# Layer norms in three steps over halved channels, a gate that normalises by tokens, and its tokens placed in three parts

## The chip, the cores and the metric

The kernel runs on one core of a Trainium2 chip. The core has a matrix engine (TensorE, PE in the profile; PEld is its loading of stationary operands), VectorE (DVE), ScalarE (ACT), GpSimd (POOL) and a sync engine (SP) that issues DMA transfers. Each engine runs its own queue of instructions in order, and semaphores make one wait for another. The metric is the device time of one execution in microseconds, the median over runs. All data is fp32.

## The reference

The input x is (2, 256, 48, 48): two images of 2,304 tokens with 256 channels, 4,608 tokens in all. Four blocks follow each other, each adding to x; what this case touches is the token-wise layer norm between them.

```python
def _ln_t(v, eps=1e-5):
    m = jnp.mean(v, axis=-1, keepdims=True)
    s = jnp.var(v, axis=-1, keepdims=True)
    return (v - m) / jnp.sqrt(s + eps)
...
    x = _L0_conv_ref(x, ...)                       # layer 0: selective scan, both directions
    x = x + _L1_conv_ref(_gn(x), ...)              # layer 1: linear attention, 3x3 convolution, MLP of 2048
    t = _to_tokens(x)
    t = t + _L2_attn_ref(_ln_t(t), ...)            # layer 2: attention of three thirds of the tokens
    t = t + _L2_ffn_ref(_ln_t(t), ...)             # 4 experts, two a token, weights from a graph
    t = t + _L3_attn_ref(_ln_t(t), L3_attn_q_weight)
    t = t + _L3_ffn_ref(_ln_t(t), ...)             # 8 experts, one a token
```

The last two, cut to what matters here:

```python
    query = jnp.einsum('bnd,de->bne', input, q_weight)
    att = jax.nn.sigmoid(jnp.einsum('bnd,bmd->bnm', query, input))
    value = jnp.einsum('bnm,bmd->bnd', att, input)
...
    logits = x @ gate_w + gate_b
    idx = jnp.argmax(probs, axis=-1)
    pos = (jnp.cumsum(one_hot, axis=0) * one_hot).sum(-1).astype(jnp.int32) - 1
    kept = pos < C                                 # C = 720 places an expert
    buf = jnp.zeros((E, C, D), dtype=h.dtype).at[idx, pos_safe].set(x, mode='drop')
```

So each token goes to its best expert, into the next free place there, in the order of the tokens. `pos` of a token depends on all tokens before it.

## The kernel before, in words

**Layout.** `E.xres`, the sum so far, and `E.xn`, its normalised copy, lie in SBUF as [128, 2, 4608]: channels on partitions in two halves of 128, tokens along the free axis. Work goes by chunks of W = 384 tokens, six a batch, twelve in all; where tokens lie on partitions, by tiles of 128 (NT = 36, three a chunk).

**The layer norm** (`layernorm`, L89 to L105; `normalize_piece` calls it for one chunk of xres into xn). As channels lie on partitions, the mean is a product with `mean_c`, a 128x128 matrix of 1/256, accumulated over the two halves (L95), which leaves the mean on every partition. VectorE subtracts it (L96), ScalarE squares (L98), two more products give the variance (L101), ScalarE takes the root (L103), VectorE the reciprocal (L104) and the product (L105). Layer 0 has a norm of its own, which isn't touched. `layernorm` runs 48 times.

**Where the norms stand.** In layer 1, `mlp(c, t1, midway)` works on one chunk in four groups g of the hidden size; `midway`, at g = 1, projects the next chunk and normalises the chunk before. Its xres comes from L646. Between chunks VectorE also sorts lists of graph edges (`sort_list`, L854 to L872). In layer 2's attention, the chunks of batch 0 are normalised two at the end of each of the three heads of batch 1; inside a head, a loop over six row tiles t makes scores (`sp`, L750), their maximum, Exp, the reciprocal of the sum, the scaled probabilities `pr` (L764) and their transposes (`tp`, L768). In layer 2's experts (`layer2_ffn`) six chunks are normalised at the start. Then expert pieces run beside the graph's work: for 8 of 12 chunks (`early`) the four experts' outputs go to DRAM (`y_d`), since the graph's weights aren't there yet. Afterwards a loop over the four other chunks takes `join` twice (it reads the pieces, VectorE weights them, GpSimd adds them into xres at L1399) with a norm after each, and `later(c)` once, which computes a chunk's experts and adds them (L1421), again with a norm.

**Layer 3's attention** (`layer3_attn`) runs, for each batch, six query chunks c against 18 key tiles i: two products `sp` (L1637), a Sigmoid (L1642), two products `po` (L1644), and at the end of a chunk L1650 adds `po` into xres. What stands in the list `behind` is issued then.

**The gate** follows the attention by chunks. `Gate.take(c)` normalises the chunk of xres into `gate_h`, transposes three tiles on TensorE with the gate's weights appended to the identity (`tg`, L1495), which gives normalised tokens and the logits' two halves in one, copies both out (L1498, L1499) and writes the tokens to DRAM (`xt_d`, L1501). `Gate.place(b)` then works on the 18 tiles of a batch: softmax, best expert, counts over tiles by two products and eight scans, and a table of which token lies in which of 8 x 720 places, built by one one-hot product a tile (`tb`, L1580, its operand `ol` from L1579). Batch 0's tiles are placed behind the first attention chunk of batch 1, batch 1's after the attention. The table's `token` (L1586) is what the first gather of layer 3's experts (`xe`, L1712, an indirect DMA by GpSimd) waits for.

The order of instructions on an engine is that of the program as a scheduler places it by data dependencies; tile pools with a fixed number of buffers set which instructions wait for an older tile's readers.

Of the kernel before, what the change touches and what calls it, by code (L numbers as in the profile page):

```python
# [8 lines left out]

# [8 lines left out]
F32 = mybir.dt.float32  # L18
# [70 lines left out]
def layernorm(E, wp, ps, src, dst, eps):  # L89

    nc = E.nc
    w = src.shape[2]
    mp = ps.tile([P, w], F32, tag="ln", name="ln_mean")
    for k in range(2):
        nc.tensor.matmul(mp, lhsT=E.mean_c, rhs=src[:, k, :], start=k == 0, stop=k == 1)  # L95
    nc.vector.tensor_tensor(dst, src, bc(mp, [P, 2, w], 1), ALU.subtract)  # L96
    sq = wp.tile([P, 2, w], F32, tag="ln_sq", name="ln_sq")
    nc.scalar.activation(sq, dst, AF.Square)  # L98
    vp = ps.tile([P, w], F32, tag="ln", name="ln_var")
    for k in range(2):  # L100
        nc.tensor.matmul(vp, lhsT=E.mean_c, rhs=sq[:, k, :], start=k == 0, stop=k == 1)  # L101
# [3 lines left out]
    nc.vector.tensor_tensor(dst, dst, bc(rs, [P, 2, w], 1), ALU.mult)  # L105

# [333 lines left out]
def normalize_piece(E, wp, ps, c, eps=1e-5):  # L440

    cs = slice(c * W, (c + 1) * W)
    layernorm(E, wp, ps, E.xres[:, :, cs], E.xn[:, :, cs], eps)
# [4 lines left out]
def layer1(ctx, E, edges):  # L448
# [78 lines left out]
    for b in range(NB):  # L527
# [79 lines left out]
        def mlp(c, t1, midway):  # L607
# [16 lines left out]
            for g in range(16 // FG):  # L624
# [3 lines left out]
                if g == 1:  # L628
                    midway()
                for m in range(2):  # L630
# [20 lines left out]
        for c in range(NCH):  # L651
# [5 lines left out]
            def midway():  # L657
                if dw is not None:
                    following.append(project(c + 1, dw))
                if b * NCH + c:  # L660
                    normalize_piece(E, lw, psn, b * NCH + c - 1)

            mlp(c, t1, midway)
# [6 lines left out]
    normalize_piece(E, lw, psn, NB * NCH - 1)  # L670
# [4 lines left out]
def layer2_attn(ctx, E):  # L675
# [46 lines left out]
    for b in range(NB):  # L722
# [8 lines left out]
        for h in range(NH):  # L731
# [11 lines left out]

            pT = act.tile([P, ST, S], F32, tag="pT", name="pT", bufs=1)
            for t in range(ST):
# [19 lines left out]
                for n in range(0, ST, 3):  # L765
# [5 lines left out]
                    else:  # L771
                        nc.vector.tensor_copy(pT[:, n : n + 3, t * P : (t + 1) * P], tp)

# [26 lines left out]

            if b:
                for c in range(2 * h, 2 * h + 2):
                    normalize_piece(E, wp, psn, (b - 1) * NCH + c)
# [499 lines left out]
def layer2_ffn(ctx, E, edges):  # L1303
# [25 lines left out]
    with (  # L1329
# [3 lines left out]
        for c in range(NCH, 2 * NCH):  # L1333
            normalize_piece(E, lw, psl, c)
# [66 lines left out]
    def later(c):  # L1401
# [6 lines left out]
        for e in range(NX):  # L1408
            gp = spread(gT, e)
            for hid in hidden(c, e):  # L1410
                pass
# [14 lines left out]
    for i in range(n_late):  # L1426
        while joined * n_late < EARLY * (i + 1):
            join(joined)
            normalize_piece(E, late, psn, joined)
            joined += 1  # L1430
        later(EARLY + i)
        if i < n_late - 1:
            normalize_piece(E, late, psn, EARLY + i)
# [3 lines left out]
class Gate:  # L1437

# [6 lines left out]
    def __init__(self, E, keep, wp):  # L1445
# [13 lines left out]
        self.lg = wp.tile([P, NT, 2, NX], F32, name="lg")  # L1459
# [23 lines left out]

    def take(self, E, c, lw, psl):

        nc = E.nc
        TG = self.TG
        h = lw.tile([P, 2, W], F32, tag="gate_h", name="gate_h")
        layernorm(E, lw, psl, E.xres[:, :, c * W : (c + 1) * W], h, 1e-5)
        xtok = lw.tile([P, TG, C], F32, tag="gate_x", name="gate_x", bufs=1)  # L1490
        for i in range(TG):
            o = slice(i * P, (i + 1) * P)
            xp = psl.tile([P, 2, P + self.NX], F32, tag="xp", name="xp", bufs=2)
            for k in range(2):
                nc.tensor.matmul(  # L1495
                    xp[:, k, :], lhsT=h[:, k, o], rhs=self.tg[:, k, :], start=True, stop=True
                )
            nc.vector.tensor_copy(xtok[:, i, :].rearrange("p (k m) -> p k m", k=2), xp[:, :, :P])  # L1498
            nc.vector.tensor_copy(self.lg[:, c * TG + i], xp[:, :, P:])  # L1499
# [3 lines left out]
        )  # L1503

    def place(self, E, b, ps):

        nc, wp = E.nc, self.wp
        NX, CAP, JT, JP, NJ = self.NX, self.CAP, self.JT, self.JP, self.NJ
        ids, ones = self.ids, self.ones
        n = NT // NB  # L1510
        bs = slice(b * n, (b + 1) * n)
        full = [P, n, NX]

        pb = wp.tile(full, F32, tag="pb", name="pb")
        nc.vector.tensor_tensor(pb, self.lg[:, bs, 0], self.lg[:, bs, 1], ALU.add)
        nc.vector.tensor_tensor(pb, pb, bc(self.gb, full, 1), ALU.add)
# [19 lines left out]
        pp = ps.tile(full, F32, tag="xp", name="pp", bufs=2)  # L1536
# [350 lines left out]
```

## Time and profile before

Three runs took 5549.81, 5555.41 and 5556.3 us. The profile is of one execution.

| what | value |
|---|---|
| median of three runs | 5555.41 us |
| the profiled execution's own time | 5556.52 us |
| its span in the profile | 5554.7 us |
| outside the span | 1.8 us |
| granted TensorE clock, mean over the span | 0.954 |
| TensorE busy | 4861.4 us (88%) |
| VectorE busy | 3476.2 us (63%) |
| ScalarE busy | 2380.4 us (43%) |
| GpSimd busy | 2388.5 us (43%) |

The page cuts the span in 40 slices of 139 us. Each digit is an engine's busy share in tenths, and `PEclk` the granted clock of TensorE in tenths of full speed:

```profile
PE   7888888887887787779999999998799999997996
DVE  4899988988999888999973234375624211212333
POOL 3888887888999888820000000078112000001112
PEclk8999999999999899999999999999899999998997
```

The first 17 slices are layer 0, where three engines share the work. Layer 1 follows up to slice 22, layer 2 with its graph up to slice 31 (GpSimd's 7 and 8 in slices 26 and 27 are the graph), layer 3's attention up to 36, its experts to the end. An engine's busy time includes time at half clock, which makes its matmuls take twice as long. The groups that are touched are small beside these: the 192 matmul records of `ln_mean` have a median of 486 ns each, and a pair of fp32 products leaves four such records.

### The profile page before, as it was taken

The page shows a single profiled execution, that of the slowest core. Times are in us where ns is not written, and L with a number is a line of the kernel's source. Part 1 is how long each engine was busy: PE and PEld are TensorE (multiplying, and loading weights), DVE is VectorE, ACT ScalarE, POOL GpSimd, SP SyncE. Part 2 cuts the span into 40 slices and gives each one's busy share as a digit, 9 for nine tenths or more (in the row PEclk, how much of TensorE's full clock was granted, in tenths as well). Part 3 has the DMA queues.
Part 4 walks back from the last instruction along what each step waited for, and adds up shares of the span by engine and source line. Part 5 has one row for each costly group of instructions (what it writes and reads, how often), then busy time and mean ns, then how long its engine had stood idle before and what let it go on. Part 6 is the DMA issues. An engine that isn't in the chain of part 4 may idle for free. (4 is left out here: it accounts for less than half of the span.)

```text
span 5554.7 us, 47440 instructions
## 1 busy us (share of the span) xinstructions
PE 4861.4 (88%) x15480; PEld 2681.8 (48%) x15480; DVE 3476.2 (63%) x5134; ACT 2380.4 (43%) x4945; POOL 2388.5 (43%) x1295
## 2 busy tenths in 40 slices
PE   7888888887887787779999999998799999997996
PEld 3444344443333343345555555565455555554664
DVE  4899988988999888999973234375624211212333
ACT  5767677666766566522222123322133222221220
POOL 3888887888999888820000000078112000001112
PEclk8999999999999899999999999999899999998997
DMA  4444554443444444321100100111011100001323
GB/s 159 165 172 170 173 178 158 162 154 143 159 160 154 165 154 157 150 80 36 49 14 0 38 1 1 51 33 24 15 55 49 35 9 6 6 9 18 85 75 79
DMA packets 173644, 486.56 MB, mean 88 GB/s; under 512 B 31487, under 2 KB 96516, under 8 KB 173124
## 3 DMA queue, kind: packets, MB, share of 16 engines
q1 hardware_dynamic: 165252, 471.82, 24.2%
q0 software_dynamic: 8128, 11.55, 1.6%
q8 instruction: 126, 2.06, 0.1%
q14 instruction: 138, 1.13, 0.1%
HBM read 416.44 MB, written 66.86 MB: 87 GB/s over the span
## 5 line engine op out<-in xcount | busy, mean ns | idle before, releaser
L332 PE MATMUL yp<-hc,ident 128*128 128x384 f32 x3072 | 1201.6, 524 | 293.4 <-DVE hc L378 252.6
L347 POOL TENSOR_TENSOR db<-dtu,bb 128x1536 f32<-128x1536 f32 x384 | 1333.0, 3472 | 49.3 <-issue 19.1
L332 PEld LDWEIGHTS yp<-hc,ident 128*128 128x128 f32 x3072 | 575.4, 198 | 876.8 <-DVE hc L378 451.6
L378 POOL TENSOR_TENSOR hc<-ho,cc 128x384 f32<-128x384 f32 x576 | 580.7, 1016 | 184.6 <-DVE ho L370 83.6
L378 DVE TENSOR_TENSOR hc<-hs,cc 128x384 f32<-128x384 f32 x960 | 497.9, 540 | 38.8 <-PE yp L332 37.6
L364 ACT ACTIVATE hs<-dt,negab 128x384 f32<-128x384 f32 x768 | 434.0, 581 | 92.5 <-DVE ho L373 41.3
L364 ACT ACTIVATE hs<-dt,negaf 128x384 f32<-128x384 f32 x768 | 433.3, 581 | 55.2 <-DVE hc L378 25.5
L373 DVE TENSOR_TENSOR_SCAN hs<-hs,state,db 128x384 f32<-128x384 f32 x400 | 394.6, 1008 | 55.8 <-POOL db L347 30.3
L370 DVE TENSOR_TENSOR_SCAN hs<-hs,state,db 128x384 f32<-128x384 f32 x400 | 395.9, 1009 | 30.2 <-POOL db L347 22.9
L1712 POOL DMA_INDIRECT xe<-xt_d,token x48 | 49.1, 1023 | 777.6 <-issue 766.2
L254 PE MATMUL mm<-xw,w_cv 128*128 128x384 f32 x768 | 288.5, 511 | 65.6 <-ACT xs L258 27.8
L1644 PE MATMUL po<-at,xtok 128*128 128x384 f32 x864 | 334.1, 508 | 7.6 <-ACT at L1642 7.6
L900 POOL PARTITION_ALL_REDUCE most<-most x1 | 0.4, 382 | 744.4 <-DVE ub L714 744.4
L1637 PE MATMUL sp<-qT,xn 128*128 128x384 f32 x864 | 312.1, 486 | 0.0
L1341 PE MATMUL ph<-xn,w 128*128 128x384 f32 x768 | 288.6, 518 | 23.3 <-issue 9.1
L1642 ACT ACTIVATE at<-sp 128x384 f32<-128x384 f32 x216 | 104.8, 491 | 465.6 <-PE sp L1637 465.5
L1650 DVE TENSOR_TENSOR xres<-xres,po 128x384 f32<-128x384 f32 x24 | 13.3, 554 | 411.0 <-PE po L1644 410.0
L633 PE MATMUL po<-hid,wfc 128*128 128x384 f32 x768 | 256.4, 488 | 0.0
L615 PE MATMUL pf<-t,wfc 128*128 128x384 f32 x768 | 255.3, 489 | 0.0
L373 DVE TENSOR_TENSOR_SCAN ho<-hs,state,db 128x384 f32<-128x384 f32 x240 | 239.6, 999 | 15.2 <-ACT hs L364 15.1
L370 DVE TENSOR_TENSOR_SCAN ho<-hs,state,db 128x384 f32<-128x384 f32 x240 | 239.3, 997 | 8.4 <-ACT hs L364 8.2
L1345 ACT ACTIVATE hid<-ph,vec 128x384 f32<-128x384 f32 x192 | 111.3, 581 | 302.7 <-PE ph L1341 243.4
(423 smaller groups left out, 8156.8 us busy)
## 6 DMA issues: line engine op xcount, KB each, us to landing
bb<-bcd SPq DMA_DIRECT2D x192, 768.0 KB
cc<-bcd SPq DMA_DIRECT2D x192, 768.0 KB
xw<-xi_d SPq DMA_DIRECT2D x24, 774.0 KB
w<-in_m_w SPq DMA_DIRECT2D x16, 1024.0 KB
y_d<-y SPq DMA_DIRECT2D x32, 384.0 KB
ye<-y_d SPq DMA_DIRECT2D x32, 384.0 KB
xi_d<-xz SPq DMA_DIRECT2D x48, 192.0 KB
z_d<-xz SPq DMA_DIRECT2D x48, 192.0 KB
```

Source lines behind the costliest of these rows:

```text
L254: nc.tensor.matmul(px, lhsT=w_cv[b, s][:, d * 4 + k, :], rhs=xw[:, d, o : o + W], start=k == 0, stop=k == 3,)
L332: nc.tensor.matmul(yp[d], lhsT=E.ident, rhs=hc, start=False, stop=summed[d] == NS)
L347: nc.gpsimd.tensor_tensor(db, bc(dtu[:, d, :], [P, GN, W], 1), bb, ALU.mult)
L364: nc.scalar.activation(hs, dt[:, d, :], AF.Exp, scale=nega[s][:, d * NS + n : d * NS + n + 1])
L370: nc.vector.tensor_tensor_scan(to, hs, db[:, j], init, ALU.mult, ALU.add)
L373: nc.vector.tensor_tensor_scan(to[:, ::-1], hs[:, ::-1], db[:, j, ::-1], init, ALU.mult, ALU.add)
L378: (nc.gpsimd if on_pool else nc.vector).tensor_tensor(hc, to, cc[:, j, :], ALU.mult)
L615: nc.tensor.matmul(pf, lhsT=wfc1[:, k, f * P : (f + 1) * P], rhs=t1[:, k, :], start=k == 0, stop=k == 1,)
L633: nc.tensor.matmul(po[m], lhsT=wfc2[:, f, m * P : (m + 1) * P], rhs=hid[:, i, :], start=f == 0, stop=f == 15,)
L1341: nc.tensor.matmul(ph, lhsT=w1[:, e, k, f * P : (f + 1) * P], rhs=xn[:, k, c * W : (c + 1) * W], start=k == 0, stop=k == 1,)
L1637: nc.tensor.matmul(sp, lhsT=xn[:, k, t0 + i * P : t0 + (i + 1) * P], rhs=qT[:, k, c * W : (c + 1) * W], start=k == 0, stop=k == 1,)
L1644: nc.tensor.matmul(po[m], lhsT=xtok[:, i, m * P : (m + 1) * P], rhs=at, start=i == 0, stop=i == MT - 1,)
```

## The change

`layernorm` becomes a generator of three steps. First, VectorE adds the two channel halves of the source into `ln_half`. Second, one product takes the mean from it, VectorE subtracts, ScalarE squares, and VectorE adds the halves of the square. Third, one product takes the variance, and root, reciprocal and scaling follow. The callers issue the steps apart: one in each group g of layer 1's mlp (through the new argument `norm`); one after each row tile in the heads of batch 1 of layer 2's attention; at the start of layer 2's experts in pairs of chunks, step by step; in `later`, one step for each hidden tile, for the chunks joined just before and the late chunk of the round before.

The gate has no such norm. `take` transposes the unnormalised chunk, and for each tile bn_stats and bn_aggr give the mean and variance of its tokens on their own partitions. The logits are corrected with the column sums of the gate's weights (`gsum`), and the tokens are normalised by one tensor_scalar a tile. `take` is a generator too, with one step a tile; the attention takes a step at every third key tile. `place` takes a range of tiles: batch 0's 18 as before, then 15 of batch 1 behind the last attention chunk, and the last three after the attention.

```diff
 def layernorm(E, wp, ps, src, dst, eps):
...
+    half = wp.tile([P, w], F32, tag="ln_half", name="ln_half")
+    nc.vector.tensor_tensor(half, src[:, 0, :], src[:, 1, :], ALU.add)
+    yield
     mp = ps.tile([P, w], F32, tag="ln", name="ln_mean")
-    for k in range(2):
-        nc.tensor.matmul(mp, lhsT=E.mean_c, rhs=src[:, k, :], start=k == 0, stop=k == 1)
+    nc.tensor.matmul(mp, lhsT=E.mean_c, rhs=half, start=True, stop=True)
     nc.vector.tensor_tensor(dst, src, bc(mp, [P, 2, w], 1), ALU.subtract)
     sq = wp.tile([P, 2, w], F32, tag="ln_sq", name="ln_sq")
     nc.scalar.activation(sq, dst, AF.Square)
+    half = wp.tile([P, w], F32, tag="ln_half", name="ln_half")
+    nc.vector.tensor_tensor(half, sq[:, 0, :], sq[:, 1, :], ALU.add)
+    yield
     vp = ps.tile([P, w], F32, tag="ln", name="ln_var")
-    for k in range(2):
-        nc.tensor.matmul(vp, lhsT=E.mean_c, rhs=sq[:, k, :], start=k == 0, stop=k == 1)
+    nc.tensor.matmul(vp, lhsT=E.mean_c, rhs=half, start=True, stop=True)
...
     nc.vector.tensor_tensor(dst, dst, bc(rs, [P, 2, w], 1), ALU.mult)
+    yield
...
                 if g == 1:
                     midway()
+                next(norm, None)
...
+            norms = [normalize_piece(E, wp, psn, (b - 1) * NCH + c) for c in range(2 * h, 2 * h + 2) if b]
...
+                if norms:
+                    next(norms[t // 3])
...
-            if b:
-                for c in range(2 * h, 2 * h + 2):
-                    normalize_piece(E, wp, psn, (b - 1) * NCH + c)
...
-        for c in range(NCH, 2 * NCH):
-            normalize_piece(E, lw, psl, c)
+        for c in range(NCH, 2 * NCH, 2):
+            for _ in zip(*(normalize_piece(E, lw, psl, c + i) for i in range(2))):
+                pass
...
             for hid in hidden(c, e):
-                pass
+                next(norms, None)
...
     for i in range(n_late):
+        done = [EARLY + i - 1] if i else []
         while joined * n_late < EARLY * (i + 1):
             join(joined)
-            normalize_piece(E, late, psn, joined)
+            done.append(joined)
             joined += 1
-        later(EARLY + i)
-        if i < n_late - 1:
-            normalize_piece(E, late, psn, EARLY + i)
+        norms = chain.from_iterable(normalize_piece(E, late, psn, c) for c in done)
+        later(EARLY + i, norms)
+        run(norms)
...
     def take(self, E, c, lw, psl):
...
-        h = lw.tile([P, 2, W], F32, tag="gate_h", name="gate_h")
-        layernorm(E, lw, psl, E.xres[:, :, c * W : (c + 1) * W], h, 1e-5)
-        xtok = lw.tile([P, TG, C], F32, tag="gate_x", name="gate_x", bufs=1)
+        xtok = lw.tile([P, TG, C], F32, tag="gate_x", name="gate_x")
...
-                    xp[:, k, :], lhsT=h[:, k, o], rhs=self.tg[:, k, :], start=True, stop=True
+                    xp[:, k, :], lhsT=E.xres[:, k, o], rhs=self.tg[:, k, :], start=True, stop=True
                 )
             nc.vector.tensor_copy(xtok[:, i, :].rearrange("p (k m) -> p k m", k=2), xp[:, :, :P])
-            nc.vector.tensor_copy(self.lg[:, c * TG + i], xp[:, :, P:])
+            nc.vector.tensor_copy(raw[:, i], xp[:, :, P:])
+            nc.vector.bn_stats(st[:, i, :], xtok[:, i, :])
+            nc.vector.bn_aggr(mv[:, i, :], st[:, i, :])
+            yield
+
+        rs = lw.tile([P, TG], F32, tag="gate_rs", name="gate_rs")
+        nc.scalar.activation(rs, mv[:, :, 1], AF.Sqrt, bias=E.eps[1e-5])
+        nc.vector.reciprocal(rs, rs)
+        full = [P, TG, NX]
+        lg = self.lg[:, c * TG : (c + 1) * TG]
+        nc.vector.tensor_tensor(lg, bc(mv[:, :, 0], full, 2), bc(self.gsum, full, 1), ALU.mult)
+        nc.vector.tensor_tensor(lg, raw[:, :, 0], lg, ALU.subtract)
+        nc.vector.tensor_tensor(lg, lg, raw[:, :, 1], ALU.add)
+        nc.vector.tensor_tensor(lg, lg, bc(rs, full, 2), ALU.mult)
+        for i in range(TG):
+            nc.vector.tensor_scalar(
+                xtok[:, i, :], xtok[:, i, :], mv[:, i, 0:1], rs[:, i : i + 1], ALU.subtract, ALU.mult
+            )
...
-    def place(self, E, b, ps):
+    def place(self, E, a, b, ps):
...
-        n = NT // NB
-        bs = slice(b * n, (b + 1) * n)
+        n = b - a
+        bs = slice(a, b)
...
-        behind = [lambda: normalize_piece(E, lw, psl, T // W - 1)]
+        gate.sums(E, psl)
+        behind = normalize_piece(E, lw, psl, T // W - 1)
...
+                    if i % 3 == 2:
+                        next(behind, None)
...
-                while behind:
-                    behind.pop(0)()
-                if c < NCH - 1 or b == NB - 1:
-                    gate.take(E, b * NCH + c, lw, psl)
...
+                run(behind)
+                behind = gate.take(E, b * NCH + c, lw, psl)
+                if c == NCH - 1 and b < NB - 1:
+                    behind = chain(behind, gate.place(E, b * n, (b + 1) * n, psl))
+                elif c == NCH - 2 and b == NB - 1:
+                    behind = chain(behind, gate.place(E, b * n, NT - gate.TG, psl))
+        run(behind)
...
-        gate.place(E, NB - 1, psl)
+        run(gate.place(E, NT - gate.TG, NT, psl))
```

## The prediction

> **What bounds the kernel now.** I read the page's 40 slices first, then a table of busy times in stages that I cut where the work changes:
>
> ```profile
> core 0: us, PE busy (x) PEld busy (x) DVE busy (x) ACT busy (x) POOL busy (x), PEclk, DMA share, GB/s
> 0.00:2400.00 2400.00, 1931.42 (x5184) 953.86 (x5184) 2109.47 (x2727) 1602.47 (x3657) 1969.54 (x992) 0.95 0.45 160
> ...
> 2460.00:3120.00 660.00, 648.93 (x2018) 376.14 (x2017) 469.61 (x880) 191.72 (x308) 0.00 (x0) 0.99 0.07 22
> 3120.00:3498.00 378.00, 357.80 (x1285) 214.69 (x1284) 144.90 (x285) 100.37 (x180) 23.23 (x24) 0.97 0.05 14
> 3498.00:3620.00 122.00, 121.09 (x391) 64.03 (x389) 40.05 (x59) 50.93 (x80) 1.80 (x4) 1.00 0.23 61
> 3620.00:4088.00 468.00, 411.02 (x2053) 263.36 (x2054) 263.95 (x306) 102.38 (x169) 233.10 (x129) 0.93 0.11 27
> 4088.00:4372.00 284.00, 272.60 (x783) 141.53 (x781) 121.30 (x123) 83.50 (x112) 60.01 (x35) 0.94 0.16 50
> 4372.00:5080.00 708.00, 694.21 (x2126) 374.40 (x2126) 104.20 (x208) 164.22 (x288) 0.00 (x0) 0.99 0.03 9
> 5080.00:5120.00 40.00, 14.42 (x61) 11.68 (x60) 23.27 (x72) 4.31 (x5) 3.07 (x4) 0.66 0.05 15
> ```
>
> The stages are the scan layer, layer 1, layer 2's attention (3120 to 3498), the first expert pieces (to 3620), the graph with pieces beside it (to 4088), the late and joined chunks (to 4372), layer 3's attention (to 5080) and the placing of tokens (to 5120). VectorE, GpSimd and TensorE share the scan layer. From 2460 on, but for the graph stage and the placing, TensorE is busy 95 to 99% of the time: there a matmul taken away shortens the stage by its slot, unless something else is late. The scan layer, the graph loop and the expert layer after 5120 issue the same instructions after the change, so I put them at nothing.
>
> The tiles ln_mean and ln_var say what a layer norm costs TensorE; the timeline gives the slot:
>
> ```profile
> L95 PE MATMUL ln_mean<-xres,mean_c x192: 486/486/649, 2552.9 to 5081.1; 128*128 128x384 f32 x192
> 4825.11 1.45 PE L95 MATMUL ln_mean<-xres,mean_c 128*128 128x384 f32 x4
> 4826.40 0.81 PE L1644 MATMUL po<-at,xtok 128*128 128x384 f32 x2
> ```
>
> 192 records are 48 norms of two products, two records each. The product pair begins at 4825.11 and its successor at 4826.40: 1.29 us, so 0.645 us for one product. L101 has 192 records too. 36 norms stay and lose two products each; the 12 of the gate lose all four. That is 120 products, 77 us at full clock.
>
> **The parts.** Each kept norm costs VectorE two 128x384 adds. L1650 is that operation: 554 ns. So 72 adds are 40 us of VectorE, whose cover has to be looked at stage by stage.
>
> *Layer 1*, 11 norms: 22 x 0.645 = 14.2 us. In this stage TensorE waits 5.8 us for the square and 4.3 us for xres, with the product behind it; the change places each step one group g of the mlp later (8 matmuls, about 5 us), so I count about half of that, 4 us, making 18. Against it stand 22 x 0.554 = 12 us on VectorE, which is 96% busy from 2460 to 2850 (372.62 of 390 us) with lists (MAX8 692 ns, MATCH_REPLACE8 675 ns). But cumulating VectorE's instructions ahead of each chunk's xres add in both orders gives 324 us before and 320 after by chunk 5, since sorting moves behind it; after 2850 VectorE is 36% busy. Bounds: -8 (all 12 us shown once against 18, with 2 us left of hiding) and -24 (14.2 plus both waits). Taken: -18.
>
> *Layer 2's attention*, 7 norms: 14 x 0.645 = 9.0 us. They move from the end of a head into its softmax loop, one step a row tile. There, three row tiles take VectorE about 7.2 us, a norm about 5.6 more, against 13 us of TensorE: near the limit. The row that tells it is the wait of the transposes for the scaled probabilities, 10.4 us in 6 cases with 2.5 the longest, which is a reciprocal (2.55 us) in front of the scaling on VectorE. Each of those stays, and each Sqrt now stands between two Exps (table load 1.28 us each way on ScalarE, 27% busy). Bounds 0 and -11, taken -6.
>
> *First pieces*, 6 norms ahead of a gapless TensorE stage: 12 x 0.645 = -7.7; in pairs, so that one's add hides beside the other's product.
>
> *Late and joined chunks*, 12 norms: 24 x 0.645 = 15.5 us. Here the clock is what I weigh:
>
> ```profile
> 4098.59 1.72 PE L95 MATMUL ln_mean<-xres,mean_c 128*128 128x384 f32 x4 [2.10 <-POOL xres L1399]
> 4100.24 2.92 PE L1389 MATMUL gp<-gT,sel 4*128 4x384 f32 x4
> ...
> 4113.77 1.45 PE L1389 MATMUL gp<-gT,sel 4*128 4x384 f32 x4
> ```
>
> The same four records take 2.92 us behind a wait of 2.10 us and 1.45 otherwise: half clock. The stage's granted 0.94 is 17 us lost to it. "TensorE: Matmul & The Clock Gate", Part 1, has half rate after an idle window of about 3.4 us. No wait here is that long (the five for GpSimd's xres add are 6.2 us in all, 2.1 the longest), so by the rule the stage owes nothing to the clock and the change is worth 15.5 us. By the row short waits do it, and taking them away could give up to 17 more. The row decides that half clock happens, but spells also begin where TensorE is listed busy, among 4-row products (gp) that stay, so I credit none. The 6.2 us wait turns into VectorE's half add waiting for GpSimd, with a hidden step of products before it is needed. Bounds: -5 (spells grow) and -22 (15.5 plus the 6.2). Taken -15.
>
> *Layer 3's attention*, 11 gate norms: 44 x 0.645 = 28.4 us. The transposes (L1495) are the same number. What is added: the placing of 15 of the second 18 tiles moves here: its `tb` products cost 0.2 us each between attention matmuls (three in 0.6 us), 3.0 us, and pp and tp 0.4. ScalarE loses a 843 ns Square and a 581 ns Sqrt a chunk, so of the 7.6 us that `po` waits for `at` I give 2; splitting the transposes adds about 1. VectorE, 15% busy, gets per chunk three bn_stats (548 ns), three bn_aggr (307) and small work, and loses a 2.55 us reciprocal: nothing. -28.4 + 3.4 - 2 + 1 = -26; bounds -20 (table loads delay `at`) and -33 (all of 7.6 gone).
>
> *The placing at the end.* The chain is told by these lines:
>
> ```profile
> 5079.42 1.20 DVE L1650 TENSOR_TENSOR xres<-xres,po 128x384 f32<-128x384 f32 x2 [39.94 <-PE po L1644]
> 5085.72 2.55 DVE L104 RECIPROCAL ln_rs<-ln_rs 128x384 f32<-128x384 f32 x1 [3.14 <-ACT ln_rs L103]
> 5092.77 0.31 DVE L1515 TENSOR_TENSOR pb<-lg 128x144 f32<-128x144 f32 x1
> 5107.24 7.11 PE L1580 MATMUL tb<-rhs,ol 128*120 128x96 f32 x36 [8.66 <-DVE pos L1590]
> 5116.01 1.01 POOL L1712 DMA_INDIRECT xe<-xt_d,token  x1 [753.54 <-issue]
> ```
>
> From xres done (5080.6) to pb 12.2 us, from pb to the gather 23.2. Changed: the first transposed tile is there after 1 us; three tiles at 1.25 us (copy, small copy, bn_stats, bn_aggr at their spacings) end at 5085.4; Sqrt, a reciprocal of three columns and four small operations at 0.21 us bring lg at 5086.6. The placing for 3 tiles instead of 18: some 40 VectorE operations at about 0.21 us, 8.4; Exp and the counts on TensorE and back, 1.8; 3 one-hot products instead of 18 (0.39 us apart), 1.5: table at 5098.3, gather 1.1 later, 5099.4, or 16.6 earlier. The xt_d write now leaves near 5087.5 instead of 5092.7, so it isn't what the gather waits for. Bounds: -8.7 (from 5080.6 to 5089.3, the norm alone) and -20. Taken -16.5.
>
> Sum: -18 - 6 - 7.7 - 15 - 26 - 16.5 = -89. The profiled execution took 5556.5 us (span 5554.7), so 5467; the median shown, 5555.4, is 1.1 lower: **5466 us**.
>
> **Rivals.** *VectorE becomes the bound in layers 1 and 2* (96% to 2850, and the softmax loop near par): these two stages give nothing, 24 less: 5490. For it: sorts in front of the adds. Against it: the cumulated orders. *The waits go as well*: every term at its far bound (24, 11, 7.7, 22, 33, 20) gives -118: 5438. For it: each named wait does stand in front of a removed product or behind a removed reciprocal. Against: waits named after one thing often pass to the next. *Slower*: each remaining product stands in TensorE's in-order queue until its half add has gone through VectorE's queue, so 72 new stalls. It decides from 89 / 72 = 1.24 us each, that is the add (0.55) plus one sort operation (0.69) in front. With 0.35 us more for half clock behind it, 1.6 each: 115 - 89, 5582. For it: the 1.9 us wait for the square has this form today. Against: in the new order 4 matmuls or more (2.6 us) stand between a step and its product nearly everywhere. *The change doesn't act*: excluded for the norms, since the built orders show 72 ln products for 192; but the end might give the norm alone, 5474.
>
> **Chances.** Forecast with its bounds 0.70; VectorE bound 0.14; waits go too 0.11; slower 0.04; nothing to be told 0.01. A measurement here can't tell less than 0.2%, 11 us, from no change. The range, 5438 to 5498, takes in both faster rivals, and 8 us above the first for a short end. Faster 0.95, same 0.02, slower 0.03: of the slower case's 0.04 a quarter would end near zero.
>
> **What would show it.** 72 records of ln_mean and of ln_var where there were 192; stages of about 642, 372, 114, 269 and 682 us, and 16 us less from xres to gather. VectorE busy some 40 us more up to 4372. New waits of TensorE for ln_half over 10 us in layer 1, or a softmax loop that waits more than 10.4 us for pr, would prove the first rival; a granted clock above 0.97 in the late chunks would show that I was wrong to credit no clock. The forecast fails if the scan layer or the graph stage moves by over 5 us.

## The result, and the profile after

The changed kernel took 5504.6 us (median of 4 runs, 5499.11 to 5506.7) against 5555.85 us for the kernel before in the same session: a ratio of 0.9908, 95% interval 0.9891 to 0.9925. Unedited on another chip it gave 0.9892 (0.9876 to 0.9909). So it is 51 us faster, where 89 were forecast, and outside the range of 5438 to 5498. The profiled execution has a span of 5502.7 us.

The same view of busy times by stage, cut at the same instructions (last addition of layer 0 and of layer 1 into xres, first and last of layer 2's attention, start of the graph loop, its last store, last late chunk, last attention chunk, first gather):

```profile
core 0: us, PE busy (x) PEld busy (x) DVE busy (x) ACT busy (x) POOL busy (x), PEclk, DMA share, GB/s
2399.20:3113.10 713.90, 679.80 (x2116) 392.39 (x2116) 535.54 (x1028) 197.12 (x325) 4.90 (x4) 0.97 0.09 30
3113.10:3191.50 78.40, 73.64 (x248) 47.11 (x249) 23.99 (x57) 3.17 (x5) 0.38 (x1) 0.74 0.21 67
3191.50:3511.70 320.20, 293.64 (x1005) 175.14 (x1003) 127.16 (x240) 101.10 (x178) 22.86 (x23) 0.95 0.00 1
3511.70:3629.00 117.30, 113.51 (x364) 60.23 (x364) 42.23 (x67) 49.61 (x78) 1.75 (x3) 0.99 0.22 64
3629.00:4100.70 471.70, 410.57 (x2053) 263.82 (x2054) 263.99 (x306) 102.61 (x169) 236.50 (x129) 0.93 0.11 27
4100.70:4361.40 260.70, 252.94 (x701) 128.88 (x699) 124.34 (x123) 80.05 (x108) 61.16 (x32) 0.92 0.15 44
4361.40:5046.20 684.80, 672.50 (x2109) 365.17 (x2109) 117.58 (x411) 158.71 (x284) 0.44 (x3) 1.00 0.04 14
5046.20:5064.20 18.00, 4.59 (x22) 3.77 (x22) 12.52 (x67) 1.80 (x3) 0.02 (x1) 0.64 0.06 22
```

The table sets these beside the same cut of the profile before. Idle is the stage's length less TensorE's busy time. The clock's loss is the sum, over steps of 1 us, of what the granted clock lacked of full speed.

| stage | before | after | change | forecast | idle before, after | clock's loss before, after |
|---|---|---|---|---|---|---|
| layer 1 | 723.2 | 713.9 | -9.3 | -18 | 29.7, 34.1 | 13.7, 18.8 |
| layer 2's weights | 68.9 | 78.4 | +9.5 | in the next | 4.3, 4.8 | 8.6, 20.5 |
| layer 2's attention | 306.2 | 320.2 | +14.0 | -6 | 14.8, 26.6 | 3.4, 17.1 |
| first pieces | 121.7 | 117.3 | -4.4 | -7.7 | 0.9, 3.8 | 0, 1.7 |
| graph beside pieces | 468.1 | 471.7 | +3.6 | 0 | | |
| late and joined chunks | 273.9 | 260.7 | -13.2 | -15 | 8.8, 7.8 | 17.1, 20.5 |
| layer 3's attention | 718.1 | 684.8 | -33.3 | -26 | 16.5, 12.3 | 5.1, 1.7 |
| placing at the end | 35.9 | 18.0 | -17.9 | -16.5 | | |

Negative changes are gains. The products are gone as counted: the tile view has 72 records each of ln_mean and ln_var.

```profile
L99 PE MATMUL ln_mean<-ln_half,mean_c x72: 486/486/1009, 2551.8 to 4372.8; 128*128 128x384 f32 x72
L107 PE MATMUL ln_var<-ln_half,mean_c x72: 486/486/987, 2562.8 to 4392.8; 128*128 128x384 f32 x72
```

Layer 2 up to the end of its attention became 23.5 us longer, where 6 us less were forecast; that is 29.5 of the 38 us that are missing. The view of TensorE's waits in the attention, after:

```profile
PE tp L782 <- DVE pr L778: 24.0, 8, 4.6
PE sp L764 <- ACT pr L773: 1.4, 2, 1.0
```

The first was 10.4 us in 6 cases before, the second 3.2 us. The four longest of the new waits for pr, 4.25 to 4.60 us, stand at heads' ends. VectorE's timeline at one of them, changed kernel:

```profile
3314.60 2.54 DVE L110 RECIPROCAL ln_rs<-ln_rs 128x384 f32<-128x384 f32 x1
3317.06 0.90 DVE L100 TENSOR_TENSOR xn<-xres,ln_mean 128x768 f32<-128x768 f32 x1
3317.87 0.15 DVE L777 RECIPROCAL sm<-sm 128x1 f32<-128x1 f32 x1
3317.94 0.94 DVE L111 TENSOR_TENSOR xn<-xn,ln_rs 128x768 f32<-128x768 f32 x1
3318.80 0.61 DVE L778 TENSOR_SCALAR pr<-pr,sm 128x768 f32<-128x768 f32 x1
```

and TensorE's:

```profile
3314.39 0.91 PE L99 MATMUL ln_mean<-ln_half,mean_c 128*128 128x384 f32 x2
3319.56 1.51 PE L782 MATMUL tp<-ident,pr 128*128 128x128 f32 x6 [4.25 <-DVE pr L778]
3320.86 1.49 PE L796 MATMUL po<-pT,xv 128*128 128x384 f32 x2
```

The scaling of a head's last row tile (L778) stands behind three operations of a norm, 4.4 us; TensorE waits 4.25 us for it, and the transposes then take 1.51 us in place of 0.85, at half clock. Before, at the same place:

```profile
3315.06 0.62 DVE L764 TENSOR_SCALAR pr<-pr,sm 128x768 f32<-128x768 f32 x1
3316.38 0.56 DVE L772 COPY pT<-tp 128x384 f32<-128x384 f32 x1 [0.70 <-PE tp L768]
3316.86 2.54 DVE L104 RECIPROCAL ln_rs<-ln_rs 128x384 f32<-128x384 f32 x1
```

```profile
3313.18 0.81 PE L101 MATMUL ln_var<-ln_sq,mean_c 128*128 128x384 f32 x2
3315.83 0.84 PE L768 MATMUL tp<-ident,pr 128*128 128x128 f32 x6 [1.84 <-DVE pr L764]
```

There the reciprocal came behind the scaling, under the `po` products. The first head, which has no norm beside it, waits at its end too. TensorE and VectorE there, kernel before:

```profile
3212.77 0.85 PE L768 MATMUL tp<-ident,pr 128*128 128x128 f32 x6 [0.61 <-DVE pr L764]
3216.10 1.51 PE L768 MATMUL tp<-ident,pr 128*128 128x128 f32 x6 [2.48 <-DVE pr L764]
```

```profile
3215.14 0.16 DVE L763 RECIPROCAL sm<-sm 128x1 f32<-128x1 f32 x1 [1.12 <-ACT pr L759]
3215.34 0.62 DVE L764 TENSOR_SCALAR pr<-pr,sm 128x768 f32<-128x768 f32 x1
```

VectorE has nothing else to do there and itself waits for Exp. So these 3.1 us (0.61 + 2.48) are the latency of a head's last row tiles, not a queue. With the waits of 1.84 us at the next four heads' ends they are the 6 cases. The 1.84 us are shorter because two products of a norm (1.29 us) lie in the gap: a product taken away at those four ends only makes the wait longer.

### The profile page after: what moved, and what is told of

The parts are those of the page before. It is cut to its first block, busy times and chain, and to the rows that moved or that the text cites. A ratio compares the mean times of both kernels' runs of the same rounds, so it can differ in the third digit from the quotient of the medians.

```text
span 5502.7 us, 47222 instructions
## 1 busy us (share of the span) xinstructions
PE 4797.7 (87%) x15246; PEld 2649.9 (48%) x15246; DVE 3499.6 (64%) x5380; ACT 2371.5 (43%) x4935; POOL 2398.4 (44%) x1295
## 5 line engine op out<-in xcount | busy, mean ns | idle before, releaser
L359 POOL TENSOR_TENSOR db<-dtu,bb 128x1536 f32<-128x1536 f32 x384 | 1333.3, 3473 | 45.5 <-issue 16.5
L382 DVE TENSOR_TENSOR_SCAN hs<-hs,state,db 128x384 f32<-128x384 f32 x400 | 397.1, 1014 | 30.0 <-POOL db L359 23.2
L266 PE MATMUL mm<-xw,w_cv 128*128 128x384 f32 x768 | 288.8, 512 | 64.5 <-ACT xs L270 26.6
L1354 PE MATMUL ph<-xn,w 128*128 128x384 f32 x768 | 292.9, 523 | 28.0 <-issue 10.4
L266 PEld LDWEIGHTS mm<-xw,w_cv 128*128 128x128 f32 x768 | 146.0, 196 | 192.7 <-ACT xs L270 43.2
```

Of the source, the lines that this page charges most:

```text
L266: nc.tensor.matmul(px, lhsT=w_cv[b, s][:, d * 4 + k, :], rhs=xw[:, d, o : o + W], start=k == 0, stop=k == 3,)
L359: nc.gpsimd.tensor_tensor(db, bc(dtu[:, d, :], [P, GN, W], 1), bb, ALU.mult)
L382: nc.vector.tensor_tensor_scan(to, hs, db[:, j], init, ALU.mult, ALU.add)
L1354: nc.tensor.matmul(ph, lhsT=w1[:, e, k, f * P : (f + 1) * P], rhs=xn[:, k, c * W : (c + 1) * W], start=k == 0, stop=k == 1,)
```

## The experiments

A chip's own time for the kernel before lay between 5507 and 5556 us in these sessions. In the profiles of the edited kernels nearly all of that difference lies in the graph stage (425 to 430 us on two chips, 465 to 472 on the others). So kernels are compared by their ratio to the kernel before on the same chip, with intervals of some 0.17% either way, and by stages of their profiles.

**e1_heads: layer 2's norms whole at the head's end again.**

```diff
-                if norms:
-                    next(norms[t // 3])
...
                     nc.gpsimd.tensor_tensor(xr, xr, y, ALU.add)
+            for norm in norms:
+                run(norm)
```

> The changed kernel with the norms of layer 2's attention whole at the end of each head again (halved products kept). If VectorE's queue in the softmax loop is what cost the time there, TensorE's wait for pr falls from 24.0 us to about 10, the stretch from the first sp to the last xres add (320.2 us in the changed kernel, 306.2 before) falls to about 300, and the whole to about 5487 us (16 to 20 us less than 5504.6). If it was the clock's chance spells there, the stretch stays within 4 us of 320.

The ratio was 0.9900 (0.9884 to 0.9917), the attention 319.3 us, the wait for pr 22.6 us. The expectation fell: this move in the program changed nothing. The waits of 4.25 us stand at four heads' ends again, with the same three operations of a norm in front of the scaling. The scheduler places instructions by their dependencies, and the norm came to stand in front of the last row tile from either place.

**e6_twoprod: the change without half adds.**

```diff
-    nc.vector.tensor_tensor(half, src[:, 0, :], src[:, 1, :], ALU.add)
...
-    nc.tensor.matmul(mp, lhsT=E.mean_c, rhs=half, start=True, stop=True)
+    for k in range(2):
+        nc.tensor.matmul(mp, lhsT=E.mean_c, rhs=src[:, k, :], start=k == 0, stop=k == 1)
```

(and the same for the variance)

> The changed kernel without half adds, each mean and variance two products again; steps, gate and placing as changed. If it is the half adds that let the scheduler draw a norm's reciprocal, subtraction and scaling on VectorE in front of a head's last row tile, layer 2's attention takes 306 us as before (320 in the changed kernel) with waits for pr of about 10 us, although it has 14 products more. If VectorE's added work is not the cause, it takes 320 + 9 = 329 us. Elsewhere 72 - 14 products more, 37 us, less what the waits in layer 1 hide: the whole 10 to 25 us above the changed kernel.

The ratio was 0.9935 (0.9916 to 0.9954), 22.5 us above the changed kernel beside it (5511.83 to 5489.29). The attention took 311.0 us with 14 products more, the wait for pr was 10.4 us in 6 cases as before, and the clock lost 3.4 us instead of 17. So it is the halving that lets the scheduler draw the norm forward; the half adds and the single products that come with them were not tried apart. The 311 us are 5 above the 306 expected: TensorE is busy 2.2 us more than before, with 8 records more in the stretch, and idle 2.6 us more (it waits 5.6 us for Exp).

**e7_po: the norms held back under the `po` products.**

```diff
+            if b:
+                z = wp.tile([P, 1], F32, tag="z", name="z")
+                nc.vector.tensor_scalar(z, ox[:, 0, 0:1], 0.0, None, ALU.mult)
+                for c in range(2 * h, 2 * h + 2):
+                    run(normalize_piece(E, wp, psn, (b - 1) * NCH + c, z=z))
```

(the first half add takes z as a third addend)

> The changed kernel with the norms of layer 2's attention held back until the head's first po product is copied (the first half add takes a zero made from that copy), so that they lie under 24 po and 8 py products in which VectorE has nothing to do. If the norm in front of the last row tile is the cause, TensorE's waits for pr fall from 24 to 3 us (the first batch's), half clock in the stretch from 34 to under 10 us, and the stretch from 320 to about 295 us; the whole 20 to 25 us below the changed kernel. If the stall only moves to the next head's start, the stretch stays above 310.

The ratio was 0.9907 (0.9891 to 0.9924), the stretch 318.3 us. The 4.25 us waits are gone, but the wait for pr is still 18.5 us in 12 cases, all of 0.61 and 2.48 us: each head ends with the latency of its last row tile, which no norm's product fills now. At the start of two heads TensorE waits 1.9 us for Exp, and one product waits 4.1 us for its half add.

**e9_ahead: the gap filled with the next head's queries.**

```diff
+                if t == ST - 1:
+                    n = b * NH + h + 1
+                    ahead = query(n // NH, n % NH) if n < NB * NH else None
                 nc.vector.reciprocal(sm, sm)
```

(`query` is the loop of pq products, moved into a function)

> The changed kernel with the next head's queries (16 records of pq, 5.2 us) issued ahead of the last row tile's transposes in layer 2's attention. If each head ends in a gap that waits for the last row tile's softmax (3.1 us of latency, 4.3 us with a norm on VectorE in front of it), the queries fill it: the waits for pr fall from 24 to under 5 us, the half clock behind them goes (34 us to under 10), and the stretch of 320 us comes to 285 to 290, 20 to 30 us below the changed kernel in the whole. If VectorE itself is the bound of the loop, the waits move to the next row tiles and the stretch stays above 312.

The ratio was 0.9843 (0.9827 to 0.9859). The windows and the waits of the stretch:

```profile
3186.10:3478.70 292.60, 282.41 (x1005) 168.99 (x1003) 127.72 (x240) 99.38 (x178) 22.86 (x23) 0.99 0.00 1
```

```profile
PE tp L791 <- DVE pr L787: 6.5, 3, 4.9
```

292.6 us for 320.2, and the granted clock 0.99 for 0.95: 16 us of idle time went, and with it half clock from 34 to 7 us. The wait and the length came out just above the expected 5 and 290 us. VectorE does the same 127 us of work in both: over the stretch it was not short of time, only its order was wrong for the gap.

**e4_pu: one-column products between the others.** Layer 2's weights stage multiplies matrices (`pg`, 512 columns) and vectors (`pu`, one column), the vectors in runs of 24.

```diff
                 for k in range(DT):
                     nc.tensor.matmul(
                         pg, lhsT=w_eo[:, k, m * P : (m + 1) * P], rhs=w_eo[:, k, :],
                         start=k == 0, stop=k == DT - 1,
                     )
+                    for j in range(2):
+                        n = 2 * m * DT + 2 * k + j
+                        q, d = n // DT, n % DT
+                        nc.tensor.matmul(
+                            pu[:, q : q + 1], lhsT=w_eo[:, d, q * P : (q + 1) * P],
...
```

> The changed kernel with the one-column products pu of layer 2's weights each put between two pg products, instead of in stretches of 24. If such a stretch counts as idle for the clock, the half-clock time between 3105 and 3192 us (41 us in the changed kernel, 17 before) falls to the one spell behind the waits at its start, 14 us or less, and the whole is about 10 us below 5504.6. If the half clock is due to the waits at the start alone or falls by chance, it stays between 17 and 41 us.

The trace of the changed kernel shows such a run. TensorE has no gap from 3138 to 3148 us, and the granted clock is 0.66:

```profile
3137.47 3.05 PE L721 MATMUL pu<-vec,w_eo 128*128 128x1 f32 x24
3138.00:3148.00 10.00, 10.00 (x31) 5.67 (x31) 2.86 (x8) 0.00 (x0) 0.38 (x1) 0.66 0.49 157
```

The ratio of e4_pu was 0.9881 (0.9865 to 0.9898), which can't be told from the changed kernel's; the stage tells. In e4_pu, and in the changed kernel's second profile (e5_again):

```profile
3110.50:3175.20 64.70, 59.54 (x248) 38.00 (x249) 23.09 (x57) 3.16 (x5) 0.38 (x1) 0.92 0.25 82
```

```profile
3106.30:3177.40 71.10, 67.05 (x248) 43.26 (x249) 23.98 (x57) 3.16 (x5) 0.38 (x1) 0.81 0.23 74
```

The same 248 records are busy for 59.5 us instead of 67, and half clock falls to 10 us. In the ten profiles of the changed kernel's order the stage took 71 to 78.5 us with 27 to 41 us at half clock, so part of the 9.5 us in the first profile was chance, and the runs of one-column products are what gives chance its opening. The kernel before has them too, with 17 us at half clock in its one profile.

**e10_pad: the late chunks' `gp` on 128 rows.** `gp` spreads a weight to all partitions with 4 rows of operand; here 124 rows of zeros are added.

```diff
-    sel = big.tile([NX, NX, P], F32, name="sel")
+    sel = big.tile([P, NX, P], F32, name="sel")
+    nc.gpsimd.memset(sel, 0.0)
...
-        gT = late.tile([NX, W], F32, tag="gT", name="gT")
-        nc.vector.tensor_copy(gT, tp)
+        gT = late.tile([P, W], F32, tag="gT", name="gT")
+        nc.vector.memset(gT, 0.0)
+        nc.vector.tensor_copy(gT[:NX], tp)
```

> The changed kernel with the products gp of the late chunks widened from 4 to 128 rows (124 of them zeros, 12 memsets of VectorE more), the same columns and number. If products that use few rows count as idle for the clock, the time lost to half clock in the late and joined chunks (20 to 32 us in seven profiles of that order) falls under 10 us and the stretch of 261 to 270 us comes to about 248. If the clock falls for the waits there (8 us in all), it stays above 17 us lost.

The ratio was 0.9845 (0.9828 to 0.9861). The late chunks, e10_pad first and e5_again below it:

```profile
4039.90:4276.10 236.20, 227.35 (x701) 127.35 (x699) 131.39 (x133) 80.37 (x108) 62.39 (x33) 0.99 0.17 49
```

```profile
4082.00:4346.20 264.20, 256.42 (x701) 130.24 (x699) 124.28 (x123) 79.95 (x109) 61.16 (x32) 0.91 0.16 44
```

701 records in both, and idle 8.9 us for 7.8, but 3.4 us lost to the clock for 23.9. The waits stayed and the half clock went, so it was not the waits. The two spells that are left, of 3.4 us each, do begin behind waits of 2.5 to 3 us. The profile before agrees: TensorE has no gap from 4167 to 4182 us, with gp among its products, and the granted clock is 1.00 in the first 7 us and 0.57 in the last 8.

The clock is 20.5 of the 28 us gained, and most of the rest is another thing. At full clock, too, a pair of gp records on 4 rows takes a slot of 0.83 us between 128-row products (4201.13 to 4201.96 in the first profile of the changed kernel), and 0.64 us on 128 rows (4071.77 to 4072.41 in e10_pad). There are 48 such pairs, so this comes to some 9 us by estimate. The expectation of 248 us lacked it.

**e8_hold and e11_hold2: sorts away from batch 1's group norm.** In layer 1, TensorE waits once for 9.9 us, at the group norm's product gv:

```profile
PE gv L528 <- DVE dv L526: 9.9, 1, 9.9
```

Before, it waited 3.8 us there for xres. e8_hold makes each sort depend on a finished chunk; e11_hold2 issues five lists early and eleven behind the group norm.

```diff
-        nc.vector.tensor_scalar(u, u, float(1 - T), 0.0, ALU.max, ALU.min)
+        nc.vector.tensor_scalar(u, u, float(1 - T), 0.0 if z is None else z, ALU.max, ALU.min)
...
+            if i > 2:
+                z = gp.tile([P, 1], F32, tag="z", name="z")
+                nc.vector.tensor_scalar(z, xb[:, 0, c * W : c * W + 1], 0.0, None, ALU.mult)
+            while n_list < (2, 4, 5, 7, 9, 11, 12, 13, 14, 15, 16, 16)[i]:
```

> The changed kernel with each list's sort held until a chunk of layer 1 is done, so that 48 instead of 70 of the MAX8 and MATCH_REPLACE8 pairs stand on VectorE ahead of batch 1's group norm. If VectorE sets the pace up to there, gv comes 8 to 10 us earlier (its wait of 9.9 us falls under 3 us), layer 1 ends about 8 us earlier and the whole is up to 8 us below the changed kernel, less what the later sorts cost. If VectorE isn't the bound there, gv stays within 2 us.

> The changed kernel with no list's sort between the second chunk of layer 1 and batch 1's group norm on VectorE (5 lists before, 11 behind it, the latter held by a zero made from a finished chunk). If the sorts that stand in front of the mlp's last additions in VectorE's queue make TensorE wait for gv, that wait (9.9 us) falls under 5 us and gv comes 5 to 8 us earlier (279 to about 272 us after layer 0). If TensorE waits for something else there, gv stays at 279.

e8_hold (0.9901, 0.9884 to 0.9917) took VectorE from 102 to 81 us of the 105 up to 2560 us and gained nothing: gv came 281.3 us after layer 0 (279.4 in the changed kernel), with a wait of 10.5 us at the same place, now in front of ln_mean. Sorts still stood in front of the mlp's last additions there, and so did a norm's reciprocal and scaling (3.5 us). e11_hold2 (0.9895, 0.9877 to 0.9914) had gv at 272.5 us and this left of the wait:

```profile
PE ln_mean L99 <- DVE dv L526: 2.8, 1, 2.8
```

In it VectorE is as busy up to 2560 us as in the changed kernel, 102 of 105 us. So the load of VectorE is not the bound; what stands in front in its queue is. In the whole time neither kernel can be told from the changed one.

**e2_l1mid and e3_pool: two other edits of layer 1.** e2_l1mid runs layer 1's norms whole at g = 1; e3_pool puts their half adds on GpSimd (`eng=nc.gpsimd`).

```diff
                     following.append(project(c + 1, dw))
+                run(norm)
...
-                next(norm, None)
```

> The changed kernel with layer 1's norms whole at midway again, at g = 1 (halved products kept). If VectorE sets the pace of layer 1 up to batch 1's group norm, its product gv still comes near 2678 us (within 2) and the whole stays within 4 us of 5504.6. If the placing of the steps is what cost, layer 1 (last xres add at 3113.1 us) ends 5 to 9 us earlier and the whole is at about 5497.

> The changed kernel with layer 1's half adds on GpSimd, which is idle there. If VectorE sets the pace up to batch 1's group norm, the 8 adds ahead of it (0.55 us each) come off: gv 4 to 5 us earlier than 2678.4 and the whole about 5 us below 5504.6. If VectorE has slack, gv stays within 1 us, and GpSimd's slower adds (1.0 us) cost up to 3 us where a product waits for one.

e2_l1mid (0.9883, 0.9867 to 0.9900) had gv at 278.6 us, where it was, and ended layer 1 4 us earlier than the first profile of the changed kernel, 2 earlier than the second: the placing of the steps is worth little. Its ratio can't be told from the changed kernel's. e3_pool (0.9914, 0.9898 to 0.9931) told nothing of VectorE's slack: products waited 6.5 us for a first half add and 5.4 for a second, and gv came 7 us later. GpSimd's first half adds took 1.0 us. Of its eleven second ones eight took 1.0 to 1.9 us and three 5.0 to 9.5, each of the three beside a row of SCALAR_TENSOR_TENSOR operations on VectorE. The longest:

```profile
2603.92 9.47 POOL L105 TENSOR_TENSOR ln_half<-ln_sq 128x384 f32<-128x384 f32 x1 [27.47 <-ACT ln_sq L103]
2603.99 8.55 DVE L596 SCALAR_TENSOR_TENSOR dw<-img,vec,dw 128x384 f32<-128x384 f32 x16
```

**e5_again, the change once more.**

> The changed kernel once more, unedited, as the measure for the three kernels beside it on this chip: between 0.9891 and 0.9925 of before. The stretch of layer 2's attention (first sp to last xres add) again 320 us with TensorE waiting about 24 us for pr, since that is the order of instructions. The half-clock time in the weights' stretch ahead of it (41 us in the first profile) is to fall anywhere between 17 and 41 us if it is chance, and to be 41 again if not.

As expected: 319.3 us and 23.9 us of waiting in the attention; 27 us at half clock in the weights' stage, so that part is chance within a band.

**e12_best, e13_before3 and e14_best2.** The edits of e4, e9 and e10 on the changed kernel; the same three on the kernel before; and e12 with e11's.

> Three edits on the changed kernel together: the one-column products of layer 2's weights between the others, the next head's queries ahead of the last row tile, and gp on 128 rows. If each does what it does alone, the weights' stretch takes 65 us (71 to 78 in the changed kernel), the attention about 288 (320), the late chunks about 248 (261 to 270): some 50 us below the changed kernel, a ratio to before near 0.981.

> The kernel before, with the same three edits as e12_best. If the forecast's shortfall lies in the gaps of the heads and in the clock of the late chunks and the weights' stretch, the change is worth more where these are mended: against e12_best the attention differs by 9 us (14 products), the late chunks by 15 to 18, layer 1 by 9, layer 3's attention by 33, the placing by 18, some 85 to 90 us in all, and this kernel stands near 0.995 of before. If the products removed in the attention were worth nothing even without a gap, the stretch is the same 293 us in both and the whole differs by under 80.

> e12_best with the sorts kept from in front of batch 1's group norm, as in e11_hold2. If the gain of 7 us at gv is kept, some 5 to 7 us below e12_best, a ratio to before near 0.977. If it is lost behind it, the same as e12_best within 3 us.

e12_best took 5391.6 us against 5506.66: 0.9785 (0.9768 to 0.9801), the fastest with e14_best2, 0.9779 (0.9763 to 0.9796). The latter reached the end of layer 1 6 us earlier, which the timed runs can't tell. e13_before3 stood at 0.9947 (0.9931 to 0.9964). So the change is worth 0.9785 / 0.9947, some 90 us by estimate, give or take 13, where gap and clock are mended, by stage: layer 1 8 us, weights 2, attention 2, first pieces 5, late chunks 24, layer 3's attention 33, placing 18. The expectation met the sum and missed two parts. The attention differs by only 1.6 us (294.5 to 292.9): TensorE is busy 6 us less, but waits 4 us more, 4.9 us of it once for pr, and has one spell of half clock; its products stay worth little while norms stand in the row tiles' queue. And the late chunks differ by 24.5 us: 16 us are busy time, mostly the removed products, and 8 us idle time, since before3 waits 14.4 us for GpSimd's additions with its ln_mean, and the changed order does not.

## Why the prediction was wrong, point by point

- **Layer 2's attention, taken as -6, measured +14: the step that failed.** The prediction read the 10.4 us of waits for pr as a norm's reciprocal (2.55 us) in front of the scaling, and went on: "Each of those stays". No such reciprocal stood there. The 2.48 us in a head without a norm are latency, near 2.55 by accident, and the other waits were short because products of the norms filled them. So the 9 us of products were not all there to be had. Then the halving changed VectorE's order, and the norm did move from behind the last row tile's scaling to in front of it. The cost: 11.8 us of idle time more and, in busy time, 9 us of half clock, against 6.7 us of products gone. The table loads that the prediction named were not it: TensorE's waits for Exp fell. The order of VectorE's instructions is fixed when the kernel is built and could have been read in front of this scaling. The sum was off as well: row tiles before follow each other at 3.33 us (3206.02 and 3209.35), so three take TensorE 10 us, not 13, against 12.8 us of VectorE.
- **The weights' stage** (+9.5) I had at nothing but its two products. Against the one profile before, the ten profiles lie 2 to 10 us higher, so part is chance; e4 shows its opening. That the stage is longer at all by the change is not shown.
- **Late and joined chunks, -13.2 for -15.** The term was sound: at full clock TensorE's busy time fell by 15.4 us, idle time by 1, and 3 us more went to half clock. The account of the clock, which moved nothing in the number, missed. The row I chose to go by read half clock as due to short waits, and I credited nothing. The Trainium skill, "TensorE: Matmul & The Clock Gate", Part 1, lets the clock fall after an idle window, but TensorE was listed busy, and e10 moved no wait. What e10 and e4 have in common is products that use few of the array's rows or columns. So 20.5 us of clock's loss stayed in the stage.
- **Layer 1, taken as -18, measured -9.3: a mis-sized term.** The products went: TensorE is busy 13.7 us less, with 1 us more of half clock in it. The 4 us from hidden waits became 4.4 us of idle time more. The waits for the square and for xres (10.1 us) went, but in their place gv waits 9.9 us and one product cx 3.8 us. I had summed VectorE's work ahead of each addition and found it no greater; e8 and e11 show that the sum was the wrong measure.
- **First pieces** -4.4 for -7.7: 3 us of new waits in a stage that had none, and 1.7 us of clock. **Graph** +3.6 for nothing: the cause stays open, and between chips this stage differs by 45 us.
- **Layer 3's attention** -33.3 for -26: busy time fell by 29 us, of which 3 were half clock, and idle time by 4. The wait for `at`, from which I took 2 us, stayed (7.6 and 7.5 us). What fell was the wait of the token transposes for `xtok` (8.2 to 3.1 us), which the sum did not have. **Placing** -17.9 for -16.5, as reckoned: the first gather started 17.4 us after the last addition ended. Its lines:

```profile
5045.57 1.20 DVE L1710 TENSOR_TENSOR xres<-xres,po 128x384 f32<-128x384 f32 x2 [5.46 <-PE po L1704]
...
5051.92 0.18 DVE L1571 TENSOR_TENSOR pb<-lg,gb 128x24 f32<-128x24 f32 x1
...
5061.00 1.51 PE L1635 MATMUL tb<-rhs,ol 128*120 128x96 f32 x6 [5.34 <-DVE rhs L1628]
...
5064.18 1.01 POOL L1770 DMA_INDIRECT xe<-xt_d,token  x1 [702.32 <-issue]
```

pb starts 5 us after the additions for 12, and the gather 12.3 us behind pb for 23.2.

The rival of VectorE as the bound in layers 1 and 2 came nearest in its mechanism (a softmax loop that waits more than 10.4 us for pr was its sign), but not in its name or size: VectorE was 40% busy there, the two layers together lost 14 us, and about half the loss in the attention was the clock.

## What to carry to other kernels

A matmul taken from a busy engine is worth its slot only where no latency gap stands at its place: look for the gap first, and fill it with work of the next round. A helper's added operation is priced by what it comes to stand in front of in its engine's queue, and where a scheduler decides that, the built order in front of each critical instruction has to be read, not the load or the line in the program. When the clock is half with the engine listed busy, look at the rows and columns that its products use; here, zeros in the unused rows were enough.

## What the runs showed of the hardware

- Products of 4 rows, and runs of 24 products of one column, bring TensorE to half clock though it is listed busy: widening the former to 128 rows with zeros took the loss in the late chunks from 20 to 32 us (ten profiles of the changed order) to 3.4 us, at the same number of records.
- Two records on 4 rows between 128-row products took 0.83 us at full clock, and 0.64 us on 128 rows.
- In most stages the loss moves in steps of 1.7 us, 3.4 us at half clock, and equal instructions differ by several steps between executions: 20.5, 22.2, 23.9, 25.6, 29.0 and 32.4 us occur in those ten profiles.
- After waits of 4.25 us or more the next transposes took 1.51 us in all four cases of the changed kernel's first profile. After the six waits of 2.48 us in e7_po they took 1.51 us twice, 1.08 once, and 0.84 or 0.85 three times. So waits of 2.5 us bring half clock only sometimes.
- GpSimd added two 128x384 tiles in 1.0 us while VectorE was idle, and in 5.0, 6.4 and 9.5 us beside rows of 9 to 16 SCALAR_TENSOR_TENSOR operations of VectorE (e3_pool). Why stays open, and the profile's spans on GpSimd are rough.
